# A graph attention layer and a graph convolution on one core: another order for the last two rounds

## The chip, the core and the metric

The kernel runs on one core of a Trainium2 chip. The metric is the device time of one execution in microseconds (us), as the median of three runs. An execution has five engines with instruction streams of their own: PE (matrix products, with PEld for its weight loads), DVE (vector), ACT (scalar), POOL and SP. PE writes its products to banks of PSUM, where DVE and ACT read them; everything else lies in SBUF.

## The reference

For 64 graphs of 256 nodes with 512 features, an attention layer and then a graph convolution, each behind a layer norm and a relu and each added to its input:

```
h = relu(layernorm(x))
q, k, v = h Wq' + bq, h Wk' + bk, h Wv' + bv
weight = adj * exp(q k');  weight = weight / rowsum(weight)
x = x + weight v
h = relu(layernorm(x))
A = adj + I;  d = rowsum(A) ** -0.5
x = x + (A * d * d') (h W + b)
```

All of it is in float32.

## The kernel before

Two graphs make a pair, and there are NP = 32 pairs. A tile `x_tiles[p]` holds 128 x 4 x 512 values: index t = 2 n + g is row half n of graph g. `block(i, n)` of it is column half i of row half n, so a pair has four blocks, and each is 128 x 512 values.

Every large product is done as seven half-size products with sums before and after them (the Strassen-Winograd scheme). A stage has a letter, and its seven products have the numbers 1 to 7: `g` is queries against the merged query-key weights, `v` values, `s` scores, `o` the weights times the values, `l` the adjacency times the normed features, and `w` the result of `l` times W. `left_sums` makes the four sums s1 to s4 of the left side (s3 overwrites a21 in place), `right_sums` those of the right side, and the stage functions add up the products as they come. An `l` product is 8 matmul instructions (x8 in the profile) on 128 x 128 pieces; a `w` product is 8 on 128 x 256, an `o` product 4.

The order of all work is written out by hand. `run(order, stages, work)` goes through a string of tokens: `l7` issues product 7 of stage l, and what `work` holds for that token is issued behind it, held back by the last reads of PSUM so far (`issue_after`). PE's instructions are chained in the order of the tokens (`in_order`, L298 in the profile). Within an engine a scheduler may still reorder what has no such tie.

The loop overlaps three pairs. The last call of `run` is different: it works off pairs p = NP - 2 = 30 and NP - 1 = 31, with small letters for what is around pair 30 and capitals `O`, `L`, `W` for the last pair's output and neighbour stages. There is nothing left to overlap with behind `L` and `W`. The names used below:

- `measure_again` (L314, L315 on DVE, L304 to L325 on POOL): mean and variance of x and from them scale and offset for the second norm (`nb_b` is the last of them).
- `second_norm` (L331): four relus on ACT that make `h_b` from x. `l1` reads row half 0 of it, `l2` row half 1.
- `find_node_sums` (L445 to L448): `left_sums` on `h_b`. For the last two pairs all four are on DVE: s1 at L445, s2 at L446, s3 (in place) at L447, s4 at L448. `l6` reads s2, `l5` s1, `l7` s3, `l3` s4.
- In `neighbour_stages`: L936 copies l1 to b11, L940 adds l2, L945 makes `U_l` = product l6 less b11 and so frees the bank that l7 adds to; L953, L954 make b22, L955 on POOL makes t2, L963 takes it less the bank of l5 and l3, L964 makes t1, L965 and L966 on POOL make t3 and t4. The `w` products read b11 (1), b21 (2), t2 (6), t1 (5), t3 (7), b22 (3), t4 (4).
- `by_way_of` adds a running sum in a bank to x by way of SBUF: two scalings on ACT (L931) and one addition on POOL (L932). `into` adds a bank to x on DVE in two instructions (L922).
- `add_graph_bias` (L397): four instructions on DVE. `add_value_bias` is a DMA. `move_weights` (L521) copies pieces of the transposed weights, for pair 31 partly on POOL; `find_weight_sums` and `find_value_sums` are POOL's sums of the `o` stage.
- `store` (L1004, L1008): writes x to DRAM, the last pair in eight pieces of 128 KB, all issued on SP.

All of yS (the seven right-hand parts of the `w` products) of pair 31 has the same buffer as pair 30's, so `L2` and what follows stand behind the `w` products of pair 30, whose last, `w4`, is put between L1 and L2:

```python
"l1 l2 l6 l5 l7 O1 l4 O5 l3 O6 O2 O7 O3 O4 w1 w2 w6 w5 w7 w3 L1 w4 "
"L2 L6 L5 L7 W1 L4 L3 W2 W6 W5 W7 W3 W4",
```

Of the kernel before, what the change touches and what calls it, by code (L numbers as in the profile page):

```python
# [9 lines left out]
F32 = mybir.dt.float32  # L10
# [6 lines left out]
def kernel(  # L17
# [35 lines left out]
    nc = tc.nc  # L53
    P = 128
    B, N, D = x.shape
    G = 2
    NP = B // G
# [6 lines left out]
    HD = D // 2  # L64
    EPS = 1e-5

    A11, A12, A22, S1, S2, S3, S4 = range(7)
# [5 lines left out]
    p1 = ctx.enter_context(tc.tile_pool(name="p1", bufs=1))  # L73
# [3 lines left out]
    ps_m = ctx.enter_context(tc.tile_pool(name="ps_m", bufs=6, space=bass.MemoryType.PSUM))  # L77
# [3 lines left out]
    sub, add, mult = ALU.subtract, ALU.add, ALU.mult  # L81
# [4 lines left out]
    def in_dram(t, p, g):  # L86
        return t[G * p + g].rearrange("(nb p) k -> p nb k", p=P)
# [39 lines left out]
    w1_set = const.tile([P, 7, 2, HD], F32, tag="w1", name="w1_set")  # L127
# [149 lines left out]
    def value_weight_steps():  # L277
# [9 lines left out]
    norms, deg, ds, terms, blocks, hTs, parts, second, sides = ({} for _ in range(9))  # L287
    flats, gTs, query_parts, weights, row_sums, turned, wTs, weight_parts, value_parts, aTs = (
        {} for _ in range(10)
    )  # L290

    measured, offsets = [], []
    last_product = [None]

    def in_order(*args, **kwargs):

        with tc.issue_after(last_product[0]) if last_product[0] else ExitStack():
            last_product[0] = nc.tensor.matmul(*args, **kwargs).ins  # L298
# [139 lines left out]
            copy = eng.tensor_copy if eng else nc.scalar.copy  # L438
            copy(dst[j * Q : (j + 1) * Q, i], src[i * Q : (i + 1) * Q, j])  # L439

    def left_sums(eng, parts_, s):

        a11, a12, a21, a22 = parts_
        s1, s2, s4 = (s[:, i] for i in range(3))
        eng.tensor_tensor(s1, a21, a22, add)  # L445
        eng.tensor_tensor(s2, s1, a11, sub)  # L446
        eng.tensor_tensor(a21, a11, a21, sub)  # L447
        last = eng.tensor_tensor(s4, a12, s2, sub)  # L448
        if eng is nc.gpsimd:
            read(last)  # L450
        return a11, a12, a22, s1, s2, a21, s4
# [124 lines left out]
        with tc.issue_after(offsets[-1]):  # L576
            find_adjacency_sums(p, False)

    def find_node_sums(p):
        h = second[p]  # L580
        hbS = p1.tile([P, 3, G, HD], F32, tag="hbS", name=f"hbS_{p}")
        a11, a12, a21, a22 = (
            h[:, j * G : j * G + G, ts(i, HD)] for i in range(2) for j in range(2)
        )
        eng = nc.gpsimd if p < NP - 2 else nc.vector
        second[p] = left_sums(eng, (a11, a12, a21, a22), hbS)

    def add_value_bias(p):
        nc.gpsimd.dma_start(
# [10 lines left out]
    def read(ins):  # L600
        last_read[ins.ins.engine] = ins.ins
        return ins

    def temp(tag, name):
        return p1.tile([P, 2, HD], F32, tag=tag, name=f"{tag}_{name}")
# [272 lines left out]
    def neighbour_stages(p):  # L878

        xt, d = x_tiles[p], deg[p][0]  # L880
        a11, a12, a22, s1, s2, s3, s4 = second[p]
        c11, c21, c22, u1, u2, u3, u4 = sides[p]
        yS = p1.tile([P, 7, 2, N], F32, tag="yS", name=f"yS_{p}")
        b11, b21, b22, t1, t2, t3, t4 = (yS[:, i] for i in range(7))
        pm, t = {}, {}

        l_banks = {}

        def gather(bank, left, right, start=False):
            if start:  # L890
                l_banks[bank] = ps_m.tile([P, 2, G, P], F32, tag="pm", name=f"pm_l_{p}_{bank}")
            for fi in range(2):
                for g in range(G):
                    in_order(
                        l_banks[bank][:, fi, g, :],
                        left[:, g, ts(fi, P)],
                        right[:, g, :],
                        start=start and fi == 0 and g == 0,
                        stop=fi == 1 and g == 1,
                        skip_group_check=True,  # L900
                    )
# [12 lines left out]

        def factor(n, r):
            return d[:, n * G + r : n * G + r + 1]

        def into(i, n, bank):
            for r in range(G):
                to = block(i, n)[:, r, :]  # L920
                read(
                    nc.vector.scalar_tensor_tensor(  # L922
                        to, bank[:, r, :], factor(n, r), to, mult, add
                    )
                )

        def by_way_of(tag, i, n):

            more = temp(tag, f"w{p}")
            for r in range(G):  # L930
                read(nc.scalar.mul(more[:, r, :], pm["w"][:, r, :], factor(n, r)))  # L931
            read(nc.gpsimd.tensor_tensor(block(i, n), block(i, n), more, add))  # L932

        def l_1():
            pm["l"] = gather(0, a11, c11, True)
            read(nc.scalar.copy(b11, pm["l"]))  # L936

        def l_2():
            side = gather(1, a12, c21, True)
            read(nc.vector.tensor_tensor(b11, side, b11, add))  # L940

        def l_6():
            gather(0, s2, u2)
            t["part"] = temp("U3", f"l{p}")
            read(nc.vector.tensor_tensor(t["part"], pm["l"], b11, sub))  # L945

        def l_5():
            pm["rest"] = gather(2, s1, u1, True)

        def l_7():  # L950
            gather(0, s3, u3)
            three = temp("A0", f"l{p}")
            read(nc.scalar.copy(three, pm["l"]))  # L953
            read(nc.vector.tensor_tensor(b22, pm["rest"], three, add))  # L954
            read(nc.gpsimd.tensor_tensor(t2, b22, t["part"], sub))  # L955

        def l_4():
            gather(0, a22, u4)
            read(nc.scalar.copy(b21, pm["l"]))

        def l_3():
            gather(2, s4, c22)
            read(nc.vector.tensor_tensor(t2, t2, pm["rest"], sub))  # L963
            read(nc.vector.tensor_tensor(t1, pm["rest"], t["part"], add))  # L964
            read(nc.gpsimd.tensor_tensor(t3, t2, b11, sub))  # L965
            read(nc.gpsimd.tensor_tensor(t4, b21, t2, sub))  # L966

        def w_1():
            pm["w"] = product(0, b11, A11, True)
            by_way_of("A1", 0, 0)  # L970

        def w_2():
            into(0, 0, product(1, b21, A12, True))

        def w_6():
            product(0, t2, S2)
            by_way_of("U2", 0, 1)

        def w_5():
            pm["w_rest"] = product(2, t1, S1, True)  # L980
            into(1, 1, pm["w_rest"])

        def w_7():
            product(0, t3, S3)
            by_way_of("U3", 1, 1)

        def w_3():
            product(2, b22, S4)
            into(0, 1, pm["w_rest"])

        def w_4():
            product(0, t4, A22)
            into(1, 0, pm["w"])

        return (
            {1: l_1, 2: l_2, 3: l_3, 4: l_4, 5: l_5, 6: l_6, 7: l_7},
            {1: w_1, 2: w_2, 3: w_3, 4: w_4, 5: w_5, 6: w_6, 7: w_7},
        )

    def store(p):  # L1000
        xt = x_tiles[p]
        if p < NP - 1:
            for g in range(G):
                nc.sync.dma_start(in_dram(out, p, g), of_graph(xt, g))  # L1004
            return
        for i, n in ((0, 0), (1, 1), (0, 1), (1, 0)):
            for g in range(G):
                nc.sync.dma_start(  # L1008
                    out[G * p + g, n * P : (n + 1) * P, ts(i, HD)], xt[:, n * G + g, ts(i, HD)]
                )  # L1010

# [105 lines left out]
    behind = ExitStack()  # L1117
# [32 lines left out]
    for p in range(NP - 2):  # L1150
# [7 lines left out]
    p = NP - 2  # L1158
    ends = later(neighbour_stages, NP - 1)
    run(  # L1160
# [3 lines left out]
        {**around(p), "O": later(output_stage, NP - 1), "L": ends, "W": ends},  # L1164
        {
            "g1": [(move_weights, p, 8, 16)],
# [7 lines left out]
            "v7": [  # L1174
                (claim, p),
                (second_norm, p),
                (find_node_sums, p),
                (move_weights, p + 1, 0, 8, nc.gpsimd),
            ],
            "v3": [(move_weights, p + 1, 8, 12)],  # L1180
            "l1": [
                (move_weights, p + 1, 12, 16),
                (find_weight_sums, p + 1),
                (find_value_sums, p + 1),
            ],
            "l3": [(add_graph_bias, p)],
            "O4": [(measure_again, p + 1)],
            "w6": [(claim, p + 1), (second_norm, p + 1), (find_node_sums, p + 1)],
            "w4": [(store, p)],
            "L7": [(add_graph_bias, p + 1)],  # L1190
            "W4": [(store, p + 1)],
        },
    )

# [38 lines left out]
```

## Time and profile before

| what | value |
|---|---|
| median of 3 runs | 1800.49 us (1799.72 to 1801.21) |
| the profiled execution | 1800.09 us, its span 1798.1 us |
| PE busy | 1783.0 us (99%), 9964 matmuls |
| DVE, ACT, POOL busy | 1328.9, 1160.7, 1200.4 us |
| granted PE clock | 1.00 |
| last PE product of the span | from 1783.50 us on in one run of 48, modelled end 1794.07 |
| last DVE instruction | ends at 1795.0 us |
| last store issued | 1795.4 us |

All times of single instructions below are us from the start of the span. A row of the timeline has start, duration, engine, line, operation, output and inputs, and in brackets how long the engine was idle before it and what ended that. The profiled execution lies 0.4 us below the median.

### The profile page before, as it was taken

The numbers are of one execution on the slowest core, as the hardware profiler recorded it, in microseconds if no ns is written. First come the engines' busy times: TensorE is split into PE (matmuls) and PEld (weight loads), VectorE is DVE, ScalarE is ACT, GpSimd is POOL, SyncE is SP. The second block draws the span as 40 slices with busy tenths as digits, with TensorE's granted clock in tenths as the row PEclk, the third lists the DMA queues.
The fourth block names the chain that finished last, engine by engine and source line by source line (L and its number), as shares of the span: only waits on it lengthen the run. The fifth ranks groups of instructions, "written<-read, shape, count | busy, mean of one in ns | idle before, by whom it ended". The sixth has DMA issues, their size and how long they took to land.

```text
span 1798.1 us, 29084 instructions
## 1 busy us (share of the span) xinstructions
PE 1783.0 (99%) x9964; PEld 1612.5 (90%) x9964; DVE 1328.9 (74%) x3056; ACT 1160.7 (65%) x2314; POOL 1200.4 (67%) x1323
## 2 busy tenths in 40 slices
PE   9999999999999999999999999999999999999998
PEld 7889998999998999989999989999899999899987
DVE  6877777767778777777677777777776777776676
ACT  3776667766677766677666777666776666776542
POOL 4567666667676676666676766776666766667763
PEclk9999999999999999999999999999999999999999
DMA  9634444344443434443444434445434444343331
GB/s 233 125 100 77 112 112 91 103 101 99 112 110 82 115 81 108 119 88 99 109 92 112 112 81 113 88 103 121 87 97 114 87 112 112 82 112 71 65 77 47
DMA packets 254594, 182.56 MB, mean 102 GB/s; under 512 B 164720, under 2 KB 185200, under 8 KB 254448
## 3 DMA queue, kind: packets, MB, share of 16 engines
q1 hardware_dynamic: 235952, 146.11, 29.5%
q0 software_dynamic: 16896, 33.56, 13.3%
q8 instruction: 79, 1.29, 0.3%
q10 hardware_dynamic: 1600, 1.05, 0.2%
q14 instruction: 67, 0.55, 0.1%
HBM read 147.07 MB, written 33.62 MB: 100 GB/s over the span
## 4 chain that ended last, share of the span: by engine, by line
PE 92%; DVE 4%; DMA 1%; ACT 1%; issue 1%; POOL 0%; ACTq 0%; DVEq 0%; POOLq 0%
PE pm_g L298 21%; PE pm_w L298 21%; PE pm_v L298 20%; PE pm_l L298 10%; PE pm_s L298 10%; PE pm_o L298 10%; DMA b_qk<-in_L_gnn_Wk_b_dram 1%; DVE st_a L314 0%; DMA dflat<-irr_d 0%; DMA drow<-dflat 0%; ACT hT L439 0%; ACT h_b L331 0%; DVE e L783 0%; DVE st_b L314 0%; ACT e L773 0%
## 5 line engine op out<-in xcount | busy, mean ns | idle before, releaser
L298 PE MATMUL pm_w<-w_set,yS 128*128 128x256 f32 x1792 | 399.2, 380 | 1.6 <-ACT U_w L931 1.3
L298 PEld LDWEIGHTS pm_w<-w_set,yS 128*128 128x128 f32 x1792 | 335.4, 190 | 45.1 <-issue 1.4
L439 ACT COPY hT<-hq 32x512 f32<-32x512 f32 x490 | 301.9, 616 | 10.5 <-DVE hq L417 2.8
L298 PE MATMUL pm_v<-v_set,hT 128*128 128x256 f32 x1024 | 236.9, 379 | 0.8 <-DVE v L734 0.7
L298 PE MATMUL pm_g<-hT,m_set 128*128 128x256 f32 x1024 | 237.3, 379 | 0.3 <-ACT hT L428 0.3
L922 DVE SCALAR_TENSOR_TENSOR x<-pm_w,irr_d,x 128x256 f32<-128x256 f32 x256 | 110.8, 474 | 164.8 <-POOL x L932 114.8
L298 PEld LDWEIGHTS pm_g<-hT,m_set 128*128 128x128 f32 x1024 | 194.3, 190 | 27.7 <-ACT hT L428 0.5
L298 PEld LDWEIGHTS pm_v<-v_set,hT 128*128 128x128 f32 x1024 | 192.0, 190 | 26.2 <-issue 1.1
L521 ACT COPY wT<-eq 32x256 f32<-32x256 f32 x504 | 202.3, 401 | 6.2 <-DVE eq L507 0.3
L298 PE MATMUL pm_v<-v_set,hS 128*128 128x256 f32 x768 | 176.3, 379 | 0.0
L298 PE MATMUL pm_g<-hS,m_set 128*128 128x256 f32 x768 | 176.2, 379 | 0.0
L298 PEld LDWEIGHTS pm_g<-hS,m_set 128*128 128x128 f32 x768 | 145.9, 190 | 19.9
L298 PEld LDWEIGHTS pm_v<-v_set,hS 128*128 128x128 f32 x768 | 143.6, 190 | 18.3
L847 POOL TENSOR_TENSOR x<-x,A_o 128x512 f32<-128x512 f32 x62 | 82.1, 1325 | 111.5 <-ACT A_o L845 108.3
L955 POOL TENSOR_TENSOR yS<-yS,U_l 128x512 f32<-128x512 f32 x32 | 40.8, 1274 | 119.5 <-DVE yS L954 111.3
L773 ACT ACTIVATE e<-e,ks 128x128 f32<-128x128 f32 x192 | 66.3, 395 | 84.0 <-DVE e L811 43.5
L298 PE MATMUL pm_l<-aT,h_b 128*128 128x128 f32 x776 | 102.9, 276 | 3.1 <-DVE U_l L945 2.7
L331 ACT ACTIVATE h_b<-x,nb_b,rs_b 128x512 f32<-128x512 f32 x128 | 93.7, 802 | 18.9 <-POOL nb_b L325 18.4
L298 PE MATMUL pm_s<-hT,gT 128*128 128x128 f32 x768 | 101.2, 275 | 2.1 <-DVE e L794 2.1
L298 PEld LDWEIGHTS pm_s<-hT,gT 128*128 128x128 f32 x768 | 97.9, 192 | 6.0 <-DVE e L794 2.9
L445 POOL TENSOR_TENSOR wS<-wT 128x256 f32<-128x256 f32 x32 | 23.4, 731 | 116.2 <-ACT wT L521 116.2
L841 DVE TENSOR_TENSOR x<-pm_o,x 128x512 f32<-128x512 f32 x128 | 87.6, 686 | 17.4 <-PE pm_o L298 17.0
(179 smaller groups left out, 3934.2 us busy)
## 6 DMA issues: line engine op xcount, KB each, us to landing
h_a<-in_x_dram SPq DMA_DIRECT2D x64, 512.0 KB, 7.1
x<-in_x_dram SPq DMA_DIRECT2D x64, 512.0 KB, 4.4
x<-in_L_gnn_Wv_b_dram POOLq DMA_DIRECT2D x32, 1024.0 KB, 10.5
out_dram<-x SPq DMA_DIRECT2D x62, 512.0 KB, 3.3
a<-in_adj_dram SPq DMA_DIRECT2D x64, 256.0 KB, 2.9
aq<-in_adj_dram SPq DMA_DIRECT2D x128, 128.0 KB, 3.6
drow<-dflat SPq DMA_DIRECT2D x32, 256.0 KB, 6.0
wv_blocks<-in_L_gnn_Wv_w_dram SPq DMA_DIRECT2D x4, 256.0 KB, 7.6
```

The costliest lines, as they stand in the source:

```text
L298: last_product[0] = nc.tensor.matmul(*args, **kwargs).ins
L331: nc.scalar.activation(h[:, t, :], xt[:, t, :], AF.Relu, bias=nb[:, t : t + 1], scale=rd[:, t : t + 1],)
L439: copy(dst[j * Q : (j + 1) * Q, i], src[i * Q : (i + 1) * Q, j])
L445: eng.tensor_tensor(s1, a21, a22, add)
L521: copy(dst[j * Q : (j + 1) * Q, i], src[i * Q : (i + 1) * Q, j])
L773: nc.scalar.activation(block(qb, kb)[:, g], scores[:, g], AF.Exp, bias=terms[p][:, t : t + 1])
L841: read(nc.vector.tensor_tensor(block(n, i), bank, block(n, i), add))
L847: read(eng.tensor_tensor(block(n, i), block(n, i), more, add))
L922: nc.vector.scalar_tensor_tensor(to, bank[:, r, :], factor(n, r), to, mult, add)
L955: read(nc.gpsimd.tensor_tensor(t2, b22, t["part"], sub))
```

## The change

It touches only the last call of `run`, that is the last 60 us or so of the program.

- **Order.** `w4` of pair 30 goes from between L1 and L2 to behind L3. The last products are W6, W5, W7, W2, W4, W3 in place of W2, W6, W5, W7, W3, W4.
- **Own buffers.** The right-hand parts of pair 31's `w` products lie in two buffers, `yA` and `yB`, on the tags gT and hq, whose last users are done; not in the buffer of pair 30's yS. `U_l` of pair 31 takes tag U2 for U3.
- **The node sums are split** into three steps. s1 and s2 stay on DVE; s3 goes to POOL (for pair 30 behind eight copies of `move_weights`, for pair 31 behind w6); s4 on DVE is issued behind l6 and L6.
- **The addition of w6 for pair 30** on POOL is held behind the offsets (`nb_b`) of the second norm of pair 31.
- **Bias.** `add_graph_bias` of pair 30 goes from behind l3 to behind L4, that of pair 31 from behind L7 to behind W6.
- **The last product**, W3, is computed in two banks of its own, one for each graph, and each is added to x as it comes; the bank that W5 filled is added earlier, at W5. Before, W3 added to that bank, and W4 was last.
- **Stores.** The eight pieces of the last pair are issued by SP and ACT in turn (graph 0 on SP, graph 1 on ACT), in the order (0,0), (1,1), (1,0), (0,1) of (i, n).

```diff
-    def left_sums(eng, parts_, s):
+    def left_sums(eng, parts_, s, steps=(0, 1, 2)):
...
+        if 0 in steps:
+            eng.tensor_tensor(s1, a21, a22, add)
+            last = eng.tensor_tensor(s2, s1, a11, sub)
+        if 1 in steps:
+            (nc.gpsimd if len(steps) == 1 else eng).tensor_tensor(a21, a11, a21, sub)
+        if 2 in steps:
+            last = eng.tensor_tensor(s4, a12, s2, sub)
...
+        if p < NP - 1:
+            yS = p1.tile([P, 7, 2, N], F32, tag="yS", name=f"yS_{p}")
+            b11, b21, b22, t1, t2, t3, t4 = (yS[:, i] for i in range(7))
+        else:
+            yA = p1.tile([P, 4, 2, N], F32, tag="gT", name=f"yA_{p}")
+            yB = p1.tile([P, 3, 2, N], F32, tag="hq", name=f"yB_{p}")
+            b11, b21, b22, t1, t2, t3, t4 = [yA[:, i] for i in range(4)] + [
+                yB[:, i] for i in range(3)
+            ]
...
+            with tc.issue_after(behind) if behind else ExitStack():
+                read(nc.gpsimd.tensor_tensor(block(i, n), block(i, n), more, add))
...
-            t["part"] = temp("U3", f"l{p}")
+            t["part"] = temp("U3" if p < NP - 1 else "U2", f"l{p}")
...
-            by_way_of("U2", 0, 1)
+            by_way_of("U2", 0, 1, offsets[-1] if p == NP - 2 else None)
...
             into(1, 1, pm["w_rest"])
+            if p == NP - 1:
+                into(0, 1, pm["w_rest"])
...
+            for r in range(G):
+                bank = ps_m.tile([P, HD], F32, tag="pm", name=f"pm_w_{p}_{3 + r}")
+                for k in range(2):
+                    in_order(
+                        bank, b22[:, k, ts(r, P)], w1_set[:, S4, k, :], start=k == 0, stop=k == 1
+                    )
+                to = block(0, 1)[:, r, :]
+                read(nc.vector.scalar_tensor_tensor(to, bank, factor(1, r), to, mult, add))
...
-        for i, n in ((0, 0), (1, 1), (0, 1), (1, 0)):
+        for i, n in ((0, 0), (1, 1), (1, 0), (0, 1)):
             for g in range(G):
-                nc.sync.dma_start(
+                (nc.sync, nc.scalar)[g].dma_start(
...
-        "l1 l2 l6 l5 l7 O1 l4 O5 l3 O6 O2 O7 O3 O4 w1 w2 w6 w5 w7 w3 L1 w4 "
-        "L2 L6 L5 L7 W1 L4 L3 W2 W6 W5 W7 W3 W4",
+        "l1 l2 l6 l5 l7 O1 l4 O5 l3 O6 O2 O7 O3 O4 w1 w2 w6 w5 w7 w3 L1 L2 "
+        "L6 L5 L7 W1 L4 L3 w4 W6 W5 W7 W2 W4 W3",
...
-                (find_node_sums, p),
+                (find_node_sums, p, (0,)),
                 (move_weights, p + 1, 0, 8, nc.gpsimd),
+                (find_node_sums, p, (1,)),
             ],
+            "l6": [(find_node_sums, p, (2,))],
...
-            "l3": [(add_graph_bias, p)],
...
-            "w6": [(claim, p + 1), (second_norm, p + 1), (find_node_sums, p + 1)],
+            "w6": [
+                (claim, p + 1),
+                (second_norm, p + 1),
+                (find_node_sums, p + 1, (0,)),
+                (find_node_sums, p + 1, (1,)),
+            ],
+            "L6": [(find_node_sums, p + 1, (2,))],
+            "L4": [(add_graph_bias, p)],
             "w4": [(store, p)],
-            "L7": [(add_graph_bias, p + 1)],
-            "W4": [(store, p + 1)],
+            "W6": [(add_graph_bias, p + 1)],
+            "W3": [(store, p + 1)],
```

More of the change, by code (lines that the diff above doesn't have):

```diff
@@ L290 @@
     )
+    node_parts = {}
     measured, offsets = [], []
@@ L439, in move @@
             copy(dst[j * Q : (j + 1) * Q, i], src[i * Q : (i + 1) * Q, j])
-    def left_sums(eng, parts_, s):
+    def left_sums(eng, parts_, s, steps=(0, 1, 2)):
         a11, a12, a21, a22 = parts_
         s1, s2, s4 = (s[:, i] for i in range(3))
[L445 to L448, printed above, removed]
+        if 0 in steps:
[5 more added lines that the diff above has]
+            last = eng.tensor_tensor(s4, a12, s2, sub)
         if eng is nc.gpsimd:
@@ L577, in adjacency_sums_behind, with find_node_sums @@
             find_adjacency_sums(p, False)
-    def find_node_sums(p):
+    node_sums = {}
+    def find_node_sums(p, steps=(0, 1, 2)):
         h = second[p]
[L581 to L584, printed above, removed]
+        if 0 in steps:
+            node_sums[p] = p1.tile([P, 3, G, HD], F32, tag="hbS", name=f"hbS_{p}")
+        quarters = [h[:, j * G : j * G + G, ts(i, HD)] for i in range(2) for j in range(2)]
         eng = nc.gpsimd if p < NP - 2 else nc.vector
-        second[p] = left_sums(eng, (a11, a12, a21, a22), hbS)
+        node_parts[p] = left_sums(eng, quarters, node_sums[p], steps)
     def add_value_bias(p):
@@ L880, in neighbour_stages @@
         xt, d = x_tiles[p], deg[p][0]
-        a11, a12, a22, s1, s2, s3, s4 = second[p]
+        a11, a12, a22, s1, s2, s3, s4 = node_parts[p]
         c11, c21, c22, u1, u2, u3, u4 = sides[p]
-        yS = p1.tile([P, 7, 2, N], F32, tag="yS", name=f"yS_{p}")
-        b11, b21, b22, t1, t2, t3, t4 = (yS[:, i] for i in range(7))
+        if p < NP - 1:
[7 more added lines that the diff above has]
+            ]
         pm, t = {}, {}
@@ L925, in into, with by_way_of @@
                 )
-        def by_way_of(tag, i, n):
+        def by_way_of(tag, i, n, behind=None):
             more = temp(tag, f"w{p}")
@@ L931, in by_way_of @@
                 read(nc.scalar.mul(more[:, r, :], pm["w"][:, r, :], factor(n, r)))
-            read(nc.gpsimd.tensor_tensor(block(i, n), block(i, n), more, add))
+            with tc.issue_after(behind) if behind else ExitStack():
+                read(nc.gpsimd.tensor_tensor(block(i, n), block(i, n), more, add))
         def l_1():
@@ L987, in w_3 @@
         def w_3():
-            product(2, b22, S4)
-            into(0, 1, pm["w_rest"])
+            if p < NP - 1:
+                product(2, b22, S4)
+                into(0, 1, pm["w_rest"])
+                return
+            for r in range(G):
[6 more added lines that the diff above has]
+                read(nc.vector.scalar_tensor_tensor(to, bank, factor(1, r), to, mult, add))
         def w_4():
```

## The prediction

> **What bounds the kernel now.** The page comes first. PE is busy in 99% of the span at full clock, so the 1740 us ahead of the change are PE's own work and none of the edits touches them.
>
> ```profile
> span 1798.1 us, 29084 instructions
> PE 1783.0 (99%) x9964; PEld 1612.5 (90%) x9964; DVE 1328.9 (74%) x3056; ACT 1160.7 (65%) x2314; POOL 1200.4 (67%) x1323
> ```
>
> What can be won is PE's idle time in the last 55 us, and what follows PE's last product. PE's timeline there shows the gaps:
>
> ```profile
> 1750.64 1.13 PE L298 MATMUL pm_l<-aT,h_b 128*128 128x128 f32 x8 [1.25 <-DVE U_l L945]
> ...
> 1753.44 1.03 PE L298 MATMUL pm_o<-vS,wS 128*128 128x256 f32 x4
> ...
> 1759.80 10.52 PE L298 MATMUL pm_w<-w_set,yS 128*128 128x256 f32 x48
> 1770.46 0.49 PE L298 MATMUL pm_l<-aT,h_b 128*128 128x128 f32 x2
> 1771.16 0.94 PE L298 MATMUL pm_l<-aT,h_b 128*128 128x128 f32 x6 [0.22 <-ACT h_b L331]
> 1773.38 1.97 PE L298 MATMUL pm_w<-w_set,yS 128*128 128x256 f32 x8 [1.29 <-ACT U_w L931]
> ...
> 1778.99 1.16 PE L298 MATMUL pm_l<-aT,h_b 128*128 128x128 f32 x8 [0.92 <-DVE U_l L945]
> ...
> 1783.50 10.57 PE L298 MATMUL pm_w<-w_set,yS 128*128 128x256 f32 x48
> ```
>
> Six w products in a row take 10.4 us, 1.73 each; an l product takes 0.89. From w1 (1759.80) to the end of the last product (1794.07) lie 34.3 us, in which 14 w and 7 l products are 24.2 + 6.2 = 30.4. So 3.7 us (with 0.15 of lag at the end) are gaps. Pair 30's l7 has another 1.25 ahead of them.
>
> The chain of waits over the same stretch tells who makes the gap at L1. It doesn't run through PE but through DVE, POOL and ACT:
>
> ```profile
> 1757.76 2.05 DVE x L397 x3
> 1759.81 0.60 DVE x L847
> ...
> 1762.85 1.29 DVE st_b L314 x2
> ...
> 1766.10 1.27 POOL x L932
> 1767.37 0.08 issue
> 1767.46 0.23 POOL irs_b L304
> ```
>
> The bias of pair 30 (L397, 2.7 us) stands on DVE ahead of pair 31's output sums; then come the statistics; and on POOL the addition of w6 (L932, to 1767.37) stands ahead of the offsets, whose statistics are done at 1765.99. Then ACT:
>
> ```profile
> 1769.59 2.93 ACT L331 ACTIVATE h_b<-x,nb_b,rs_b 128x512 f32<-128x512 f32 x4 [3.57 <-POOL nb_b L325]
> 1772.42 0.81 ACT L931 ACTIVATE U_w<-pm_w,irr_d 128x256 f32<-128x256 f32 x2
> ```
>
> The relus end at 1772.5, two us after PE ran out of w products. w4 of pair 30 then waits for ACT's scaling of w7 (L931), which is queued behind the relus: that is the gap of 1.29. The last view is SP's timeline:
>
> ```profile
> 1786.06 9.73 SPq L1008 DMA_DIRECT2D out_dram<-x  x8
> ```
>
> The last DVE instruction ends at 1795.0, but the eighth store is issued at 1795.4, since six of the eight come one behind the other on SP from 1793.0 on, up to 0.5 us each.
>
> **The change part by part.** I walk forward with the rows' durations; the same walk over the kernel before gives its last DVE end as 1794.8 to 1795.0 where the trace has 1795.0.
>
> *Pair 30, l7 and O5.* DVE loses L447 (0.8) and does L448 (0.8) after L945. So L940 starts when l2 is done (about 1747.6, was 1749.03), L945 at 1748.5, and l7 at about 1749.3: 1.3 earlier. s3 is now one POOL instruction (1.27, L447's row on POOL for other pairs). It stands behind the eight weight copies, which end at 1748.16 now, at about 1747.5 with one DVE addition less between them; s3 ends about 1748.8, in time. But POOL's sums for the o stage move behind it: s3, then both value sums, then the weight sums, so the first weight sum, at 1749.48 before, ends at 1752.5 to 1752.7, and O5 waits for it: 1752.7 against 1753.44. Of the 1.3 a gain of 0.7 is left. What bounds it is how POOL and DVE get in each other's way. A DVE addition with both inputs in SBUF waits while POOL's addition runs:
>
> ```profile
> 1773.32 1.27 POOL L932 TENSOR_TENSOR x<-x,U_w 128x512 f32<-128x512 f32 x1 [3.76 <-ACT U_w L931]
> ```
> ```profile
> 1773.56 1.58 DVE L446 TENSOR_TENSOR hbS<-hbS,h_b 128x512 f32<-128x512 f32 x1
> 1775.06 0.68 DVE L447 TENSOR_TENSOR h_b<-h_b 128x512 f32<-128x512 f32 x1
> ```
>
> Alone it takes 0.68, beside POOL's it ends 0.55 after POOL's. With none of that O5 gains 1.3; with two such turns more on POOL (0.55 each) it is 0.4 later than before. I take 0.7, since only L448 and the output addition L847 meet POOL there, and keep -1.3 to +0.4. w1 then starts at 1759.1.
>
> *Pair 31's statistics.* The bias of pair 30 leaves this place (2.7), but the additions L847 now meet POOL's t3 and t4 (two turns, up to 1.2), and the chain's head, L963, is about 0.5 later, behind POOL's longer queue. Statistics begin about 1 us earlier (1761.8 to 1762.3). They end 2.7 later, and POOL's offsets follow at once for L932 now stands behind them (1.45 of waiting gone); these take 2.1. Relus begin at about 1766.7 and end at 1769.7, where they ended at 1772.5. U_w of w7 follows on ACT by 1770.6 and holds up nobody: w4 is now far behind.
>
> *From L1 on.* PE comes to L1 at 1759.1 + 10.4 = 1769.5 and finds its half of h_b there, L2 too. L6 needs s2: L445 at 1769.75, L446 at 1770.5, done 1771.1, where PE is at 1771.3: no wait to 0.5. At L7 the new order costs something: L940 can't start before L2 is done and two L922 (w3) are ahead of it, so L945 ends 0.3 to 0.4 behind L5. pm_l's copy to b11 (L936) no longer waits for w4 (2.15 on ACT before), because of the own buffers. w4 behind L3 covers the sums that W6 needs: L963 stands behind four bias instructions (2.7 us, from about 1776), ends about 0.6 before PE is through with w4. That cover is thin; without it, W6 would wait one bias instruction (0.7) or two. Pair 31's bias, 1.3 + 1.3 us around its wait for POOL's addition of w6, and the six L922 of W5 and W2 are done about 0.8 us before W4 ends, so they cost nothing. Gaps from w1 to the end are thus 1.0 (0.5 at L6, 0.35 at L7, the lag) against 3.7: 2.7 gained; bounds 2.0 to 3.2.
>
> *The end.* Two banks for W3 mean one L922 instead of two behind the last matmul: 0.88 becomes 0.44, so 0.44 gained. A product of 8 matmuls in two halves costs PE nothing (same count). Storing from two queues removes SP's backlog: 0.4, bounds 0.2 and 0.45 (an issue on ACT at the start of the program took 0.55, on SP 0.51).
>
> Sum: 0.7 + 2.7 + 0.44 + 0.4 = 4.2. The profiled execution goes from 1800.09 to 1795.9, its span to 1793.9; the median was 0.4 above the profiled one, so 1800.5 - 4.2 = 1796.3. What a measurement of this kernel can tell from no change is about 0.2%, 3.6 us.
>
> **The rivals.**
>
> *POOL first.* For pair 31, s3 on POOL and s2 (L446) on DVE become free at the same moment, both behind L445: DVE's dependent instruction starts 0.04 to 0.14 after the one before ends (L445 to L446 at 1729.6, L940 to L945 at 1778.2), POOL 0.08 after DVE (L963 to L965). If POOL comes first, L446 ends at about 1772.4, L6 waits 1.3 longer and all behind it: a gain of 2.9, 1797.6. The Trainium skill, SBUF — State Buffer, section "SBUF: two separate sides", says that GpSimd and such a DVE instruction share a port pair under an exclusive lock: who starts first keeps it for the whole instruction. The rows above agree, and by that rule a difference moved from DVE to POOL is no free move, here and at O5. Nothing in the trace says who wins a dead heat: 0.28.
>
> *The head gains nothing.* POOL's sums take two turns more, O5 is 0.4 late, so +0.4 for -0.7 and 1.1 of the gain is gone: 1797.4. Against it: only two DVE additions fall into that window. 0.14.
>
> *The ACT queue lands late.* The only such transfers on ACT's queue in this trace are in the first 3 us; the small one took 9.6 us to land (SP's 7.8), the last stores on SP 1.8. If the last store, issued at about 1790.8 on ACT, took 9.6, it would land at 1800.4 and the span would end 0.9 later (as now: 1795.4 + 1.8 to 1798.1), at 1801.3: 1803.7. It decides from 6.4 us on. Against it: at the start megabytes were ahead of it, here nothing. 0.04.
>
> *The order moves but the time comes back elsewhere* (W6 behind the bias, DVE's backlog under W4): the margins of 0.6 and 0.8 would have to fail together; 1799.5 to 1801, 0.04.
>
> **How the numbers follow.** My own case has 0.50, with 1795.3 to 1797.1 from its bounds. The range takes in the first two rivals with half a us for their sizes: 1795.2 to 1798.5. Faster by over 3.6 us is my case but for its upper part, with a little of the first two: 0.57. Within 3.6 us: those two, the last, and half of the third: 0.40. Slower: 0.03.
>
> **What would show it.** Right: on PE l7 of pair 30 at about 1749.3, a wait at O5 for POOL's wS, no wait for U_w at all, relus of pair 31 from about 1766.7, L1 and L2 in one run of 16 behind the w products, waits at L6 and L7 under 0.6, W6 without a wait, the last store issued within 0.1 of the last DVE instruction. Wrong: L446 of about 1.8 us beside L447 on POOL and a PE wait of 1.5 or more at L6 (first rival); O5 later than 1753.4 (second); a last store of over 3 us (third); W6 released by L963.

## The result, and the profile after

The changed kernel takes 1795.59 us (median of 12 runs, 1794.87 to 1796.68) where the kernel before took 1800.34 beside it (1799.59 to 1801.21): a ratio of 0.9975, 95% interval 0.9967 to 0.9982, or 4.75 us less. The forecast was 1796.3 and a gain of 4.2. The profiled execution took 1795.94.

The first lines of the page say that PE's work is what it was, 1783 us:

```profile
span 1793.9 us, 29087 instructions
PE 1783.1 (99%) x9964; PEld 1613.4 (90%) x9964; DVE 1328.7 (74%) x3056; ACT 1160.8 (65%) x2314; POOL 1204.3 (67%) x1325
```

One thing has to be settled before rows of two runs are set side by side. The first score products (`pm_s`) start at 86.05 us in the trace of before, at 86.51 in that of after, and between 85.53 and 86.76 over all runs of this study, although the work ahead of them is the same; of the 0.46 between before and after, 0.42 is still there at pair 30's l1. So I compare one **stage**: from pair 30's l1 (the first `pm_l` run of 16) to the end of the span. Before it is 1798.1 - 1745.59 = 52.51 us, after it 1793.9 - 1746.01 = 47.89: 4.62 less. Spans are given to 0.1, so a stage is good to about 0.1; a second profile of the changed kernel (experiment 9) has 47.84. "Aligned" below means 0.42 subtracted from a time of after.

The line numbers of the changed kernel are somewhat higher. PE's L298 is L299, the node sums s1 to s4 (L445 to L448) are L447, L448, L450 and L452, L945 is L959 (`U_l`), L963 is L977, the output sums L841 and L847 are L846 and L852, the bias is L398, `into` is L935 (L922), `by_way_of` L944 and L946 (L931, L932), and the last store is L1035; what lies ahead of the node sums moves by one. The experiments shift some of them by a few lines more.

PE's timeline after (start, duration, then what ran, and in brackets the wait ahead of it):

```profile
1746.01 1.95 PE L299 MATMUL pm_l<-aT,h_b 128*128 128x128 f32 x16
...
1749.79 1.13 PE L299 MATMUL pm_l<-aT,h_b 128*128 128x128 f32 x8
...
1752.85 1.13 PE L299 MATMUL pm_o<-vS,wS 128*128 128x256 f32 x4
...
1759.24 10.52 PE L299 MATMUL pm_w<-w_set,yS 128*128 128x256 f32 x48
1769.61 1.95 PE L299 MATMUL pm_l<-aT,h_b 128*128 128x128 f32 x16
1771.75 2.02 PE L299 MATMUL pm_l<-aT,hbS 128*128 128x128 f32 x16 [0.20 <-DVE hbS L448]
1773.93 1.13 PE L299 MATMUL pm_l<-aT,h_b 128*128 128x128 f32 x8 [0.16 <-DVE U_l L959]
...
1780.14 1.89 PE L299 MATMUL pm_w<-w_set,yB 128*128 128x256 f32 x8
...
1788.77 1.89 PE L299 MATMUL pm_w<-w_set,yA 128*128 128x256 f32 x8
```

The waits of 1.25, 0.22, 1.29 and 0.92 of before are gone; 0.20 ahead of L6 and 0.16 ahead of L7 are left. A bracket counts from the modelled end of the product before. One w product follows the next after 1.73 and ends after 1.89, so PE's own pace is about 0.16 ahead of that end: by the starts, L6 comes 0.35 and L7 0.39 later than two l products at 0.895 each would allow. One wait has no bracket on PE. O5 starts 1.23 behind l4, 0.34 more than an l product takes, and PE's weight loads (PEld) say what it waited for, POOL's first weight sum:

```profile
1752.85 0.73 PEld L299 LDWEIGHTS pm_o<-vS,wS 128*128 128x128 f32 x4 [0.28 <-POOL wS L447]
```

L1 and L2 are one run of 16 straight behind the w products, and W6 (1780.14) starts without a wait. The stage splits at w1 and at the end of the last product:

| part | before | after | less |
|---|---|---|---|
| l1 to w1 (the head) | 14.21 | 13.23 | 0.98 |
| w1 to the end of the last product | 34.27 | 31.42 | 2.85 |
| from there to the end of the span | 4.03 | 3.24 | 0.79 |

The chain of waits after, in the same stretch as before, still goes through DVE, POOL and ACT, but without the bias and without an addition ahead of the offsets:

```profile
1760.94 1.21 DVE x L846 x2
...
1762.18 1.29 DVE st_b L315 x2
...
1764.78 0.23 DVE mv_b L316 x2
...
1765.09 0.23 POOL irs_b L305
...
1767.22 2.94 ACT h_b L332 x4
```

From the last statistics (1765.01) to the offsets is 0.08 now, where it was 1.47 before (1765.99 to 1767.46), behind the w6 addition; the relus start at 1767.22, aligned 2.8 earlier than before. Last, the end as the timelines of DVE, ACT and SP have it:

```profile
1790.70 0.48 DVE L1016 SCALAR_TENSOR_TENSOR x<-pm_w,irr_d,x 128x256 f32<-128x256 f32 x1 [0.38 <-PE pm_w L299]
```
```profile
1791.22 0.34 ACTq L1035 DMA_DIRECT2D out_dram<-x  x1
```
```profile
1788.05 2.63 SPq L1035 DMA_DIRECT2D out_dram<-x  x4
```

One half addition of 0.48 follows the last matmul, and the last store is issued on ACT 0.04 after it, at 1791.22, with four stores on each queue.

### The profile page after: what moved, and what is told of

It reads as the page before. It is cut to its first block, busy times and chain, and to the rows that moved or that the text cites. A ratio compares the mean times of both kernels' runs of the same rounds, so it can differ in the third digit from the quotient of the medians.

```text
span 1793.9 us, 29087 instructions
## 1 busy us (share of the span) xinstructions
PE 1783.1 (99%) x9964; PEld 1613.4 (90%) x9964; DVE 1328.7 (74%) x3056; ACT 1160.8 (65%) x2314; POOL 1204.3 (67%) x1325
## 3 DMA queue, kind: packets, MB, share of 16 engines
q8 instruction: 79, 1.29, 0.3%
q10 hardware_dynamic: 2176, 1.58, 0.3%
## 4 chain that ended last, share of the span: by engine, by line
PE 93%; DVE 3%; DMA 1%; ACT 1%; POOL 1%; issue 1%; ACTq 0%; DVEq 0%; POOLq 0%
PE pm_g L299 21%; PE pm_w L299 21%; PE pm_v L299 20%; PE pm_l L299 10%; PE pm_s L299 10%; PE pm_o L299 10%; DMA b_qk<-in_L_gnn_Wk_b_dram 1%; DVE st_a L315 0%; DMA dflat<-irr_d 0%; DMA drow<-dflat 0%; ACT hT L440 0%; ACT h_b L332 0%; DVE e L788 0%; DVE st_b L315 0%; ACT e L778 0%
## 5 line engine op out<-in xcount | busy, mean ns | idle before, releaser
L299 PE MATMUL pm_w<-w_set,yS 128*128 128x256 f32 x1736 | 386.6, 380 | 0.3 <-DVE yS L977 0.3
L299 PEld LDWEIGHTS pm_w<-w_set,yS 128*128 128x128 f32 x1736 | 324.9, 190 | 42.3 <-DVE yS L977 0.7
L299 PE MATMUL pm_g<-hT,m_set 128*128 128x256 f32 x1024 | 238.0, 380 | 0.0
L299 PE MATMUL pm_v<-v_set,hT 128*128 128x256 f32 x1024 | 236.9, 379 | 0.8 <-DVE v L739 0.7
L935 DVE SCALAR_TENSOR_TENSOR x<-pm_w,irr_d,x 128x256 f32<-128x256 f32 x256 | 110.7, 475 | 159.5 <-POOL x L946 114.9
L299 PEld LDWEIGHTS pm_g<-hT,m_set 128*128 128x128 f32 x1024 | 195.0, 191 | 27.4 <-issue 0.5
L299 PEld LDWEIGHTS pm_v<-v_set,hT 128*128 128x128 f32 x1024 | 191.9, 190 | 26.2 <-issue 1.1
L299 PE MATMUL pm_v<-v_set,hS 128*128 128x256 f32 x768 | 176.3, 379 | 0.0
L299 PE MATMUL pm_g<-hS,m_set 128*128 128x256 f32 x768 | 176.2, 379 | 0.0
L299 PEld LDWEIGHTS pm_g<-hS,m_set 128*128 128x128 f32 x768 | 145.9, 190 | 19.8
L299 PEld LDWEIGHTS pm_v<-v_set,hS 128*128 128x128 f32 x768 | 143.6, 190 | 18.3
L852 POOL TENSOR_TENSOR x<-x,A_o 128x512 f32<-128x512 f32 x62 | 82.3, 1328 | 111.4 <-ACT A_o L850 108.1
L299 PE MATMUL pm_s<-hT,gT 128*128 128x128 f32 x768 | 101.2, 275 | 2.1 <-DVE e L799 2.1
L299 PEld LDWEIGHTS pm_s<-hT,gT 128*128 128x128 f32 x768 | 97.9, 192 | 6.0 <-DVE e L799 2.9
L299 PE MATMUL pm_l<-aT,h_b 128*128 128x128 f32 x776 | 102.4, 275 | 0.7 <-DVE U_l L959 0.7
L447 POOL TENSOR_TENSOR wS<-wT 128x256 f32<-128x256 f32 x32 | 23.4, 730 | 116.1 <-ACT wT L525 116.1
L846 DVE TENSOR_TENSOR x<-pm_o,x 128x512 f32<-128x512 f32 x128 | 87.8, 688 | 17.3 <-PE pm_o L299 16.9
```

The lines of the kernel that those rows point to most:

```text
L846: read(nc.vector.tensor_tensor(block(n, i), bank, block(n, i), add))
L852: read(eng.tensor_tensor(block(n, i), block(n, i), more, add))
L935: nc.vector.scalar_tensor_tensor(to, bank[:, r, :], factor(n, r), to, mult, add)
```

## The experiments

Except for experiment 6, the interval of each ratio overlaps that of the changed kernel. What tells the kernels apart is the stage, of one profile each; the medians move the same way.

**1. Stores on one queue.** The order of the pieces stays, only ACT's queue is left out.

```diff
-                (nc.sync, nc.scalar)[g].dma_start(
+                nc.sync.dma_start(
```

> The changed kernel with all eight last stores issued by SP again (order of the pieces as changed). Theory, a backlog of issues on SP: SP issues take 0.4 to 0.5 us each; (1,1) is free at about 1788.0, (1,0) at 1789.8, and the last two pieces, free at 1790.3 and 1791.2, are then issued at about 1791.3 and 1791.75, so the span ends 0.2 to 0.5 us later than with two queues. Rival, the order of the pieces and the earlier W2 and W5 already emptied the queue and the second queue adds nothing: 0.0 to 0.1 later. A landing on ACT's queue that is later than on SP's would show as a gain here.

Median 1796.12, ratio to before 0.998 [0.9971, 0.9989]; the stage takes 48.16, 0.27 more than after. SP's timeline has all eight stores:

```profile
1787.43 3.76 SPq L1035 DMA_DIRECT2D out_dram<-x  x8
```

They end 0.65 behind the last DVE instruction (1791.19 against 1790.54), where after has 0.38 (1791.56 against 1791.18) and before 0.79 (1795.79 against 1795.0). So the second queue is worth 0.27 of the 0.41 by which this tail fell; the other 0.14 goes with what stays changed here. The two banks of the last product are not it (0.37 with one bank, in experiment 2), so the order of products and pieces is left, which was not tried alone.

**2. The last product in one bank.** `W3` adds to the bank that W5 filled, as before; place in the order and queues stay.

```diff
-            if p == NP - 1:
-                into(0, 1, pm["w_rest"])
...
-            if p < NP - 1:
+            if True:
                 product(2, b22, S4)
```

> The changed kernel with W3 added to the bank that W5 filled, and that bank taken to x by two instructions behind W3 (as before), everything else as changed. Theory: behind the last matmul two DVE instructions of 0.44 us instead of one: the last DVE end 0.4 us after where it is, the span 0.4 longer. Rival: the store's landing hides it, span within 0.1.

Median 1795.9, ratio 0.998 [0.9971, 0.9989]; the stage 48.31, 0.42 more. DVE's last row is two instructions again:

```profile
1790.00 0.88 DVE L935 SCALAR_TENSOR_TENSOR x<-pm_w,irr_d,x 128x256 f32<-128x256 f32 x2 [0.85 <-PE pm_w L299]
```

0.88 for 0.48: the difference is the 0.4 of the stage, as expected.

**3. Pair 30's bias back behind l3.**

```diff
+            "l3": [(add_graph_bias, p)],
...
-            "L4": [(add_graph_bias, p)],
```

> The changed kernel with the bias of pair 30 back behind l3, ahead of pair 31's output sums on DVE. Theory, the statistics of pair 31 and with them its relus decide when L6 starts: DVE gets 2.7 us more ahead of the statistics; a part is taken back because the additions of the output sums no longer meet t3 and t4 on POOL (about 1 us), so the relus end 1.5 to 2.5 later than 1770.15, L6 waits as much more, and the span is 1.3 to 2.3 longer. Rival, PE's own order sets L6 and the relus have slack: under 0.5 longer.

Median 1797.0, ratio 0.9986 [0.9977, 0.9995]; the stage 49.65, 1.76 more. The relus start 23.01 behind l1 where after has 21.21, 1.80 later, and PE waits at three places:

```profile
1769.63 1.19 PE L299 MATMUL pm_l<-aT,h_b 128*128 128x128 f32 x8 [0.22 <-ACT h_b L332]
1771.04 0.94 PE L299 MATMUL pm_l<-aT,h_b 128*128 128x128 f32 x6 [0.22 <-ACT h_b L332]
1772.58 2.02 PE L299 MATMUL pm_l<-aT,hbS 128*128 128x128 f32 x16 [0.61 <-DVE hbS L448]
```

The bias takes 2.72 but delays the statistics by only 1.47 (17.64 behind l1 for 16.17), and DVE's timelines say why. After has, without the bias:

```profile
1757.88 1.38 DVE L852 TENSOR_TENSOR x<-x,A_o 128x512 f32<-128x512 f32 x1
...
1759.79 1.16 DVE L852 TENSOR_TENSOR x<-x,U_o 128x512 f32<-128x512 f32 x1
```

Behind the bias they are:

```profile
1759.58 0.68 DVE L852 TENSOR_TENSOR x<-x,A_o 128x512 f32<-128x512 f32 x1
...
1760.78 0.68 DVE L852 TENSOR_TENSOR x<-x,U_o 128x512 f32<-128x512 f32 x1
```

Without the bias those two additions run into POOL's t3 and t4; behind it they take 0.68 each, so 1.18 of the gain is paid back as turns. That is the "up to 1.2" of the prediction. The other 0.33 of the relus' delay goes to one addition of a `w` product of pair 30 (L935, 0.45), which now stands ahead of the last aggregate.

**4. Who wins the dead heat: an instruction more in DVE's way.** A 128x32 memset between s1 and s2 of pair 31 was to let POOL's s3 start first.

```diff
...
+                with tc.issue_after(first.ins):
+                    first = nc.vector.memset(idle, 0.0)
+            with tc.issue_after(first.ins):
+                last = eng.tensor_tensor(s2, s1, a11, sub)
```

> The changed kernel with a DVE memset of 128x32 between s1 and s2 of pair 31's node sums, so that s3 on POOL is issued ahead of s2 on DVE (the two were 0.04 us apart, DVE first). Theory, the engine that starts first keeps the other out for its whole instruction: s2 ends about 0.55 after POOL's 1.24, at 1772.75 instead of 1771.6, L6 waits 1.3 instead of 0.2, the span is 1.1 to 1.3 longer. Rival, both share and each is only slowed a little: s2 ends with the memset's length (0.1) later, the span is 0.1 to 0.3 longer.

A miss: the order did not turn. Median 1795.71, ratio 0.9977 [0.9968, 0.9986]; stage 47.83. DVE's and POOL's timelines:

```profile
1769.32 0.69 DVE L449 TENSOR_TENSOR hbS<-h_b 128x512 f32<-128x512 f32 x1 [2.95 <-ACT h_b L332]
1769.97 0.09 DVE L452 MEMSET idle<- 128x32 f32 x1
1770.05 0.69 DVE L454 TENSOR_TENSOR hbS<-hbS,h_b 128x512 f32<-128x512 f32 x1
```
```profile
1770.09 1.78 POOL L456 TENSOR_TENSOR h_b<-h_b 128x512 f32<-128x512 f32 x1 [2.55 <-DVE idle L452]
```

The memset cost nothing: s2 starts 0.73 behind the start of s1 here (1770.05 - 1769.32) and in after (1770.91 - 1770.18). It fitted into the distance that s2 keeps from s1 anyway. POOL's start did not move either, 0.77 behind that of s1 in both. The profile puts POOL's release down to the memset; by these times it was still s1. So the edit did not do what it was made for, and it says nothing on the price of losing the race.

**5. s2 behind the two additions of w3.** Here POOL's s3 starts first for certain.

```diff
-            last = eng.tensor_tensor(s2, s1, a11, sub)
+            if 4 not in steps:
+                last = eng.tensor_tensor(s2, s1, a11, sub)
+        if 3 in steps:
+            last = eng.tensor_tensor(s2, s1, a11, sub)
...
-                (find_node_sums, p + 1, (0,)),
+                (find_node_sums, p + 1, (0, 4)),
...
+            "w3": [(find_node_sums, p + 1, (3,))],
```

> The changed kernel with s2 of pair 31's node sums placed on DVE behind the two additions of w3, so that it comes to its turn at about 0.6 after s3 has begun on POOL (the memset did not turn their order round, s2 still started 0.04 ahead). Theory, POOL's instruction keeps DVE's out until it ends: s2 takes about 1.2 instead of 0.69 and ends 0.55 after POOL's, L6 starts 1.1 to 1.2 later than in the changed kernel, the stage from pair 30's l1 on is 1.0 to 1.3 longer. Rival, no such lock: s2 takes 0.69, L6 is 0.6 later, the stage 0.5 to 0.6 longer.

Median 1796.5, ratio 0.9978 [0.9968, 0.9988]; the stage 48.81, 0.92 more. POOL's, DVE's and PE's timelines:

```profile
1770.32 1.27 POOL L453 TENSOR_TENSOR h_b<-h_b 128x512 f32<-128x512 f32 x1 [2.54 <-DVE hbS L447]
```
```profile
1770.95 1.19 DVE L451 TENSOR_TENSOR hbS<-hbS,h_b 128x512 f32<-128x512 f32 x1
```
```profile
1772.29 2.02 PE L299 MATMUL pm_l<-aT,hbS 128*128 128x128 f32 x16 [1.36 <-DVE hbS L451]
```

POOL's 1.27 run through, and DVE's s2 ends 0.55 behind them, at 1772.14. L6 starts 2.74 behind the start of s1, where after has 1.57: 1.17 later, as expected. But the two w3 additions are done ahead of s2 here, so the 0.16 ahead of L7 goes, and of the 1.17 the stage keeps 0.92 (just under the 1.0 that I expected). This is the rival "POOL first" but for the place of those two additions. With them behind s2, as in the changed kernel, nothing would have to come back at L7; its price is then up to 1.2, an estimate from the 1.17 at L6, near the 1.3 of the forecast.

**6. The offsets behind the w6 addition again.** The statistics stay where they are; what POOL does of the norm is issued at w6, and the tie is taken away.

```diff
-            "O4": [(measure_again, p + 1)],
+            "O4": [(measure_again, p + 1, 1)],
...
+                (measure_again, p + 1, 2),
...
-            by_way_of("U2", 0, 1, offsets[-1] if p == NP - 2 else None)
+            by_way_of("U2", 0, 1)
```

> The changed kernel with POOL's addition of w6 (pair 30) ahead of the offsets of pair 31's norm, as before the change. Theory, that addition is on the way to the relus: it needs ACT's scaling, which ends at about 1765.5, and runs to 1766.8, so the offsets begin 1.7 to 1.8 later, the relus too, L6 waits 1.7 longer and the stage from pair 30's l1 on is 1.4 to 1.8 longer. Rival, the statistics on DVE come last and the order on POOL is worth little: under 0.5.

Median 1798.86, ratio 0.9992 [0.9983, 1.0002]; the stage 50.70, 2.81 more: the number was missed. The relus are 1.80 later (23.01 behind l1), as expected. The rest is at L6:

```profile
1774.30 2.02 PE L299 MATMUL pm_l<-aT,hbS 128*128 128x128 f32 x16 [1.77 <-DVE hbS L457]
```

In this kernel one w3 addition stands on DVE between s1 and s2, as in the kernel before; s2 then came 0.24 behind POOL's s3 and took 1.58. That is much like experiment 5's order: 1.8 + 0.9 = 2.7. Why the addition stands there is not shown; the later relus alone do not do it, for in experiment 3 they are as late (23.01) and s2 follows s1 directly.

**7. All node sums on DVE in one go again.**

```diff
-                (find_node_sums, p, (0,)),
+                (find_node_sums, p),
                 (move_weights, p + 1, 0, 8, nc.gpsimd),
-                (find_node_sums, p, (1,)),
...
-            "l6": [(find_node_sums, p, (2,))],
...
-                (find_node_sums, p + 1, (0,)),
-                (find_node_sums, p + 1, (1,)),
+                (find_node_sums, p + 1),
...
-            "L6": [(find_node_sums, p + 1, (2,))],
```

> The changed kernel with all four node sums on DVE in one go for both pairs, s3 too, as before the change. Theory, s3 and s4 stand ahead of the sums that free the banks of l7 and L7: l7 1.2 to 1.4 later and L7 1.0 to 1.2 later; O5 no longer waits for POOL, which gives back 0.3 to 0.4 at the first. The stage from pair 30's l1 on is 1.6 to 2.2 longer. Rival, POOL's queue was the tighter one and its relief gives most back: under 0.8.

Median 1797.21, ratio 0.9983 [0.9974, 0.9992]; the stage 49.72, 1.83 more. l7's wait of before is back, and a second one of that kind at L7:

```profile
1750.43 1.13 PE L299 MATMUL pm_l<-aT,h_b 128*128 128x128 f32 x8 [1.25 <-DVE U_l L959]
...
1775.10 1.16 PE L299 MATMUL pm_l<-aT,h_b 128*128 128x128 f32 x8 [1.36 <-DVE U_l L959]
```

w1 starts 14.21 behind l1, as before. So the whole head (0.98) is the split of the sums, s3 on POOL and s4 behind l6 together; the two were not tried apart.

**8. w4 between L1 and L2 again.**

```diff
-        "l1 l2 l6 l5 l7 O1 l4 O5 l3 O6 O2 O7 O3 O4 w1 w2 w6 w5 w7 w3 L1 L2 "
-        "L6 L5 L7 W1 L4 L3 w4 W6 W5 W7 W2 W4 W3",
+        "l1 l2 l6 l5 l7 O1 l4 O5 l3 O6 O2 O7 O3 O4 w1 w2 w6 w5 w7 w3 L1 w4 L2 "
+        "L6 L5 L7 W1 L4 L3 W6 W5 W7 W2 W4 W3",
```

> The changed kernel with w4 of pair 30 between L1 and L2 again. Theory, w4 hides the sums that W6 needs, and at its old place it waits for ACT's scaling behind the relus (0.45) and delays L2: without it behind L3, W6 waits for L963's place in the queue behind the bias, 1.0 to 1.5, and the stage from pair 30's l1 on is 1.0 to 1.5 longer. Rival, PE does the same work in another order and only the wait for the scaling counts: 0.3 to 0.5.

Median 1796.95, ratio 0.9982 [0.9972, 0.9992]; the stage 49.23, 1.34 more:

```profile
1770.06 1.97 PE L299 MATMUL pm_w<-w_set,yS 128*128 128x256 f32 x8 [0.34 <-ACT U_w L944]
...
1780.53 1.97 PE L299 MATMUL pm_w<-w_set,yB 128*128 128x256 f32 x8 [1.21 <-DVE yB L977]
```

The larger wait is at W6, whose sum L977 stands behind pair 30's bias: w4 covers it in the changed order.

**9. The changed kernel again, and with less on POOL.** In the second kernel pair 30's t2 goes to DVE, and pair 31's value sums are issued behind l4.

```diff
-            read(nc.gpsimd.tensor_tensor(t2, b22, t["part"], sub))
+            read((nc.vector if p == NP - 2 else nc.gpsimd).tensor_tensor(t2, b22, t["part"], sub))
...
             "l1": [
                 (move_weights, p + 1, 12, 16),
                 (find_weight_sums, p + 1),
-                (find_value_sums, p + 1),
             ],
+            "l4": [(find_value_sums, p + 1)],
```

> The changed kernel once more, beside the two others of this call. Both theories: the stage from pair 30's l1 to the span's end takes 47.9 us within 0.2 again, O5 waits some 0.4 for POOL's wS, L6 0.2 for s2.

> The changed kernel with POOL relieved around O5: t2 of pair 30 (L969) goes from POOL to DVE, and the value sums of pair 31 are issued behind l4 instead of in l1, so that on POOL s3 is followed by the weight sums. Theory (what is left of the head is POOL's queue): O5's wait of 0.3 to 0.4 goes, the statistics of pair 31 start 1 to 2.5 earlier, L6's wait of 0.2 goes; the stage from l1 to the span's end is 0.4 to 0.8 shorter than 47.9. Rival (DVE and POOL take turns, and PE's other gaps at l7 and L7 stay): what goes at O5 comes back at l7 or O6, and the stage is within 0.1 of 47.9 or longer.

The changed kernel: 1795.89, ratio 0.9978 [0.9969, 0.9987], stage 47.84. With less on POOL: 1794.46, ratio 0.9971 [0.996, 0.9982]; its stage is 1792.2 - 1745.13 = 47.07, 0.77 less than beside it and 0.82 less than the first profile of after. The intervals of the two ratios overlap, so it is the stage, not the median, that tells them apart. PE's timeline from w1 to L7 has no wait left:

```profile
1758.15 10.52 PE L299 MATMUL pm_w<-w_set,yS 128*128 128x256 f32 x48
1768.51 1.95 PE L299 MATMUL pm_l<-aT,h_b 128*128 128x128 f32 x16
1770.29 2.00 PE L299 MATMUL pm_l<-aT,hbS 128*128 128x128 f32 x16
1772.27 1.13 PE L299 MATMUL pm_l<-aT,h_b 128*128 128x128 f32 x8
```

O5 has no wait left (w1 comes 13.02 behind l1 for 13.23), and the relus start 19.91 behind l1 for 21.21, 1.3 earlier, so s2 is done before PE reaches L6. Most of what the changed kernel left over hung on POOL's queue, and the rival falls; the two edits were not tried apart. From w1 to the end of the last product it takes 30.86, and the products alone, 14 at 1.7275 and 7 at 0.895, take 30.45. This version has the shortest stage of all runs here.

**10. One edit alone in the kernel before: pair 30's bias behind L6.**

```diff
-            "l3": [(add_graph_bias, p)],
...
-            "w4": [(store, p)],
+            "L6": [(add_graph_bias, p), (store, p)],
```

> The kernel before with one edit of the change alone: pair 30's bias moves from behind l3 to behind L6, its store with it; the order of the products, the node sums, the buffers, the last product and the store queues stay as before. Theory (the bias sets the statistics and so the relus, the w6 addition only joins it): POOL's offsets get ahead of the w6 addition by themselves, the relus end about 3 earlier, w4's wait of 1.29 and the 0.22 at L1 go, up to 0.5 comes back at W6 behind two biases on DVE; the stage from pair 30's l1 to the span's end is 2.0 to 3.2 shorter than 52.5. Rival (bias, w6 addition, w4's place and the buffers each hold the gap by themselves): under 1 shorter.

Median 1797.39, ratio 0.9988 [0.9979, 0.9996]; the stage is 1796.2 - 1746.25 = 49.95, 2.56 less than before. POOL's and ACT's timelines show how:

```profile
1764.95 0.23 POOL L304 TENSOR_SCALAR irs_b<-mv_b 128x4 f32<-128x4 f32 x1 [0.38 <-DVE mv_b L315]
...
1767.00 1.27 POOL L932 TENSOR_TENSOR x<-x,U_w 128x512 f32<-128x512 f32 x1
```
```profile
1767.08 2.93 ACT L331 ACTIVATE h_b<-x,nb_b,rs_b 128x512 f32<-128x512 f32 x4 [0.41 <-POOL nb_b L325]
```

The statistics start 1.47 earlier behind l1 (15.79 for 17.26). That puts them ahead of the w6 addition, which now follows the offsets with no tie, and the relus are 3.17 earlier: 1.47 from the bias, 1.70 from the overtaking. w4's wait and the one at L1 are gone with w4 in its old place; 0.46 is left at L7 (it was 0.92). The 0.5 that I allowed at W6 did not come: in the old order W2 stands ahead of it. From w1 to the end of the last product it takes 31.69, where before has 34.27 and after 31.42: in this stretch the bias alone brings 2.58 of the 2.85.

## Why the prediction was right, step by step

- **Head, 0.7 said, 0.98 measured.** s3 on POOL started at 1747.50 aligned (said 1747.5), l7 at 1749.37 (1749.3), the first weight sum ended at 1752.38 (1752.5 to 1752.7), O5 came at 1752.43 (1752.7). The mechanism is as told: l7 gains 1.3, and POOL's longer queue takes some back at O5, though less than said. Of POOL's two value sums one was stretched (1.60 for 1.28, by L452); that is the one turn that came ahead of O5. Experiment 7 shows that the split makes the whole of it, experiment 9 that O5's wait goes when POOL has less ahead of the weight sums. POOL's timeline of after has the stretched sum and the weight sum behind it:

```profile
1750.51 1.60 POOL L536 TENSOR_TENSOR vS<-v,vS 128x512 f32<-128x512 f32 x1
1752.08 0.72 POOL L447 TENSOR_TENSOR wS<-wT 128x256 f32<-128x256 f32 x1
```

- **Gaps from w1 on, 2.7 said, 2.85 measured.** Statistics began at 1761.76 aligned (said 1761.8 to 1762.3, with the two turns of L852 as told), the relus at 1766.80 (1766.7), L6 waited 0.20 (0 to 0.5), L7 0.16 (0.35), W6 nothing; its sum was done 0.5 ahead of it (said 0.6). By the products' 30.45, the gaps went from 3.8 to 1.0; the prediction subtracted 30.4 from 34.3 and wrote 3.7, where it is 3.9. The 1.0 of after is what was said (0.5, 0.35 and the lag): it is made of 0.35 at L6, 0.39 at L7, 0.07 at W1 and 0.16 of lag. So the slip made the term too small by about the 0.15 that was measured more. What the prediction did not see is how much hangs on one edit: experiment 10 has 2.58 of the 2.85 from the bias alone, and there the offsets get ahead of the w6 addition without being tied. All the other edits together add 0.27 to that in this stretch.
- **Last product, 0.44 said, 0.42 measured** (experiment 2).
- **Stores, 0.4 said, 0.41 measured from the last DVE instruction to the last issue, of which the second queue is 0.27** (experiment 1). That the size came out is partly luck: it was put down to the queue alone, which is worth 0.27.
- Together 4.2 said and 4.6 measured in the stage.

The rivals. *POOL first* did not happen: s2 started 0.04 ahead of s3. DVE's and POOL's timelines of after:

```profile
1770.18 0.69 DVE L447 TENSOR_TENSOR hbS<-h_b 128x512 f32<-128x512 f32 x1 [2.95 <-ACT h_b L332]
1770.91 0.69 DVE L448 TENSOR_TENSOR hbS<-hbS,h_b 128x512 f32<-128x512 f32 x1
```
```profile
1770.95 1.78 POOL L450 TENSOR_TENSOR h_b<-h_b 128x512 f32<-128x512 f32 x1 [2.54 <-DVE hbS L447]
```

Its price is 0.9 to 1.2 (experiment 5), so it would have given some 1796.5 to 1796.8 and not 1797.6 (which was 1.3 on top of the forecast of 1796.3). Whoever starts first keeps the other waiting: s3 alone takes 1.27 and here 1.78, s2 alone 0.69 and in experiment 5 1.19. The Trainium skill, SBUF — State Buffer, section "SBUF: two separate sides", calls that an exclusive lock for the whole instruction. Both rows agree with it, in both orders, but for 0.14: s2 ends 0.55 behind s3 and s3 1.13 behind s2, each 0.14 less than it takes alone. *The head gains nothing* fell with O5 1.0 earlier. *ACT's queue lands late* fell too: the median from issue to landing was 2.0 us on ACT and 1.9 on SP. Of *the order moves but time comes back elsewhere* one half showed, and only with w4 back between L1 and L2: W6 then waits 1.21 (experiment 8), where the prediction had said one bias instruction (0.7) or two for a W6 that w4 does not cover.

The parts, undone one by one from the changed kernel, cost 0.27, 0.42, 1.76, 2.81, 1.83 and 1.34: 8.4 together for a gain of 4.6, since the bias, the offsets, the sums and w4's place all meet in the same waits at L6, L7 and W6. Done alone, the bias (behind L6 there, behind L4 in the changed kernel) is worth 2.56, more than half of the whole, and the offsets get ahead of the w6 addition with no tie. In the old order w4 had no wait any more once the bias was moved; whether its move is worth anything without the other edits was not tried. Not undone alone were the own buffers, the new order of W2 and W4, and the later bias of pair 31.

The dead heat went to DVE by 0.04 to 0.05 in all eight profiles in which s2 and s3 both wait for s1 alone, experiment 4 among them: counted from the start of s1, s2 starts after 0.72 or 0.73 and POOL's s3 after 0.77 or 0.78. The prediction had no ground for this beyond its 0.28 for the other way round, so that it came out is luck as far as the forecast goes. What would turn it is open; experiment 4 did not.

## What to carry to other kernels

Where a chain of small steps on several engines feeds the matrix engine, look for long work on those engines that nobody waits for (here a bias of 2.7 us on DVE) and put it behind the chain; that alone was more than half of this gain, and it let another step (POOL's offsets) overtake by itself. Parts that meet in one wait can't be added up from undoing each; do one alone as well. A sum moved to POOL brings its turns with DVE and its queue with it, so look at the next POOL result that someone waits for (here the first weight sum ahead of O5).

## What the runs showed that I had not expected

- The first score products were reached between 85.53 and 86.76 us in thirteen profiles of kernels whose work in the first 1700 us is the same, and the spans differ by that: comparing stages was good to 0.1 us, comparing spans to about 1.
- An addition on DVE with both inputs in SBUF costs 0.68, or 1.2 to 1.8 when it meets one on POOL: a long bias of 2.72 put ahead of two of them cost the statistics only 1.47.
- Stores on ACT's queue landed as fast as on SP's (2.0 against 1.9 us).
- A 128x32 memset of 0.09 us between two dependent DVE additions cost nothing (the second starts 0.73 behind the start of the first with it and without) and did not let POOL in.
